# Layer 0's strips regrouped by head, and one ring of eight wide buffers, in a two-layer graph-attention kernel

## The chip, the cores and the metric

The kernel runs on one core of a Trainium2 chip. The metric is the device time in microseconds (us) from the first to the last instruction of one execution. The kernel before took 4317.61 us, the median of three runs (4312.24 to 4321.88). The execution that was recorded with a profile took 4314.55 us, and its span in the trace is 4312.8 us; all times of instructions below are from that execution.

## The reference

Eight graphs of 2048 nodes with 256 features go through two attention layers, each with a residual and a layer norm. All graphs share one adjacency matrix.

```python
def layer0(x, adj, prior, W, a_src, a_dst, beta_tilde, W_out):      # prior = adj here
    x_proj = jnp.einsum('bnd,hdf->bhnf', x, W)                      # 8 heads of 32
    e_src = jnp.einsum('bhnf,hf->bhn', x_proj, a_src)
    e_dst = jnp.einsum('bhnf,hf->bhn', x_proj, a_dst)
    e = leaky_relu(e_src[..., :, None] + e_dst[..., None, :], 0.2)
    e = e + (softplus(beta_tilde) * jnp.log(prior + 1e-6))[:, None, :, :]
    attn = softmax(where(adj > 0, e, finfo.min))
    h = jnp.einsum('bhij,bhjf->bhif', attn, x_proj)
    return h.transpose(0, 2, 1, 3).reshape(B, N, D) @ W_out.T
def layer1(x, adj, W1, W2, W3):
    e = leaky_relu((x @ W1) @ (x @ W2).T, 0.2)
    attention = softmax(where(adj > 0, e, -1e12))
    return relu(attention @ (x @ W3))
x = layernorm(x + layer0(x, ...)); x = layernorm(x + layer1(x, ...))
```

## The kernel before

Layer 0 is done with the scores transposed: the neighbours j lie on the partitions, the queries i along the free axis. The heads are taken in pairs (`hp`, four per graph), and the neighbours in 16 tiles of 128 (`jt`). One pair with one tile is a strip (`step`, from L343), and there are 64 strips per graph, 512 in all. For each of its two heads, called a and b below, a strip makes a weight tile `s` of 128 x 2048 on VectorE (L378): the larger of a query row `c` and a neighbour factor `re`, times the masked prior `mt`. Then TensorE multiplies with it: `products` (L407) adds into the accumulator `val` (128 x 1024, two PSUM banks) with the projected features `v` as weights 32 columns wide, and into `den` with the neighbour factors alone, for the softmax's divisor. The four column groups of the array work side by side: group q has head q % 2 and half q // 2 of its queries, and each of the two banks holds 512 of those 1024 queries. So every round of four matmuls, one per group, reads the tiles of both heads.

For some strips (the table `SUMMED`, by graph and pair) the divisor isn't summed on TensorE. There, ScalarE starts two tiles `d` with a scaled copy of `s` (L395), VectorE adds the later ones of the chain (L389), and in the pair's last strip TensorE reduces both tiles at once with weights of ones. The `d` tiles have two buffers.

After a pair's last strip, `finish` (L414) empties the accumulators with ScalarE: two copies of 64 x 1024 take `val` into `ht` (L423), which holds all heads' rows of a graph as node tile by feature, and one copy of 128 x 1024 takes `den` (L426). The rest of `finish` goes on in later strips: reciprocals by way of HBM (`rec_d`), their rows broadcast back (`rb`, 128 x 1024), and every second pair a multiplication of `ht` by them (L452). `val` and `den` have one buffer each, so the next pair's first matmuls wait for these copies.

When the four pairs of a graph are done, `output` (L455) takes groups of four node tiles through the output projection (`y`, L480), adds the input rows into the same columns of `ht` (L482), and normalizes them there (L483 to L489). A group has two `y` tiles. `turn` (L494) transposes the result into `x1t` and makes layer 1's values `h3`. Layer 1 (`Dot`) then takes 16 rows of 128 queries. A row's scores `e` go through ScalarE into `p` (L545), VectorE adds the mask and takes the row's extreme (L548), ScalarE applies exp in place (L551), and in the next row's turn TensorE transposes `p` (`pt`, L569), with ScalarE copying each transpose out (L571), and multiplies by `h3` into `acc` (L585). The tile `p` is one buffer of 128 x 2048 for the whole kernel.

The tiles `s` rotate through six buffers of 128 x 2048. At the start the same buffers hold the input rows and the tiles `m` from which `mt` is made. Tiles named "mm" (`y`, `e`, `pt`, `tr` and the like) rotate through three PSUM banks.

The first graph's layer 0 runs alone (0 to about 480 us), with the other graphs' projections in between. From then on layer 1 of one graph is interleaved with layer 0 of the next. The order on TensorE is the program's own, and that on the SyncE queue from the second part on; on VectorE and ScalarE a scheduler fixes the order when the program is built. The interleaving puts 4 + 2 strips of the next graph ahead of the output stage, 2 after each of its first groups, then 2 + 2, and the other 44 over 13 rows of layer 1, three or four after each row's `acc`. A graph's strips 16, 32, 48 and 64 end a pair. Strip 16 is followed by transposes and by the start of layer 1; strips 32 and 48 are followed at once by strips of the next pair; strip 64 is followed by a row of layer 1. The last graph's layer 1 runs alone from about 4000 us.

Of the kernel before, what the change touches and what calls it, by code (L numbers as in the profile page):

```python
# [27 lines left out]
def kernel(  # L28
# [40 lines left out]
    SUMMED += [[(2, 4, 10, 13)] + [tuple(range(0, NT, 2))] * (NP - 1)] * (B - 2)  # L69
# [10 lines left out]
    p_all = whole.tile([P, N], F32, tag="p", name="p")  # L80

    def mm_tile(name):
        return ps.tile([P, BK], F32, tag="mm", name=name)

# [42 lines left out]
    first_x = [wide.tile([P, NT // 2, D], F32, tag="s", name="xr", bufs=6) for _ in range(2)]  # L127
# [36 lines left out]
    rec_d = dram.tile([B, NP // 2, 2, 2, 2, HALF], F32, name="rec_d")  # L164
# [8 lines left out]
    def transpose_x(xg, dst):  # L173
        for kc in range(KC):
            t = mm_tile("tr")
            for k in range(IG):
                nc.tensor.transpose(t[:, ts(k, P)], xg[:, k, ts(kc, P)], ident)
            nc.scalar.copy(dst[:, kc, :], t)  # L178

    def make_m(jt):  # L180
# [3 lines left out]
        m = wide.tile([P, NT, P], F32, tag="s", name="m", bufs=6)  # L184
# [51 lines left out]
    class Gat:  # L236
# [12 lines left out]
        def scores_first(self, xt):  # L249
# [3 lines left out]
            for kc in range(KC):  # L253
                for q in range(NB):
                    nc.tensor.matmul(t[ts(q, DH), :], wp[:, kc, D:], xt[:, kc, ts(q, BK)],
                                     start=(kc == 0), stop=(kc == KC - 1))
# [8 lines left out]
        def row(self, it, xt, v, scores=True):  # L265
# [3 lines left out]
            for kc in range(KC):  # L269
                nc.tensor.matmul(t[:, 0:cols], xt[:, kc, ts(it % IG, P)], wp[:, kc, 0:cols],  # L270
# [72 lines left out]
        def step(self, count=1):  # L343

            for _ in range(count):
# [29 lines left out]
                for a in range(HP):  # L375
                    h = hp * HP + a
                    sa = wide_tile("s", "s", 6)
# [13 lines left out]
                self.products(self.val, [v[:, jt, ts(a, DH)] for a in range(HP)], s, jt == 0, jt == NT - 1)  # L391
# [4 lines left out]
                if jt not in chain:  # L396
                    self.products(self.den, [e[:, jt, h:h + 1].to_broadcast([P, DH]) for h in heads], s,
                                  jt == min(set(range(NT)) - set(chain)),
                                  not chain and jt == NT - 1)
                if chain and jt == NT - 1:  # L400
                    self.products(self.den, [ones] * HP, self.sums, False, True)
# [5 lines left out]
        def products(self, dst, weights, s, start, stop):  # L407
            for c in range(HALF // BK):
                for q in range(4):
                    nc.tensor.matmul(dst[ts(q, DH), ts(c, BK)], weights[q % 2],  # L410
                                     s[q % 2][:, ds(q // 2 * HALF + c * BK, BK)],
                                     start=start, stop=stop)

        def finish(self, hp):  # L414
# [4 lines left out]
            if hp == 0:  # L419
                self.ht = whole.tile([P, NT, KC, P], F32, tag="heads", name="ht")  # L420
            ht = self.ht[:, :, hp // 2, :]
            for s in range(2):
                nc.scalar.copy(ht[lo:lo + HP * DH, ts(s, NT // 2), :],  # L423
                               self.val[ts(s, HP * DH), :].rearrange("p (t i) -> p t i", i=P))
# [8 lines left out]
            for s in range(2):  # L433
                nc.sync.dma_start(rec_d[b, hp // 2, s, hp % 2].rearrange("a (p c) -> (a p) c", c=HALF // DH),
# [5 lines left out]
            for s in range(2):  # L440
# [4 lines left out]
                for a in range(2 * HP):  # L445
                    nc.sync.dma_start(rb[ts(a, DH), :],
                                      rec_d[b, hp // 2, s, a // HP, a % HP:a % HP + 1, :].to_broadcast([DH, HALF]))
                rbs.append(rb)
                yield
            for s, rb in enumerate(rbs):  # L450
                half = ht[:, ts(s, NT // 2), :]
                nc.vector.tensor_mul(half, half, rb.rearrange("p (t i) -> p t i", i=P))  # L452
                yield

        def output(self):  # L455
# [13 lines left out]
            for g in range(NB):  # L469
# [5 lines left out]
                z = self.ht[:, ts(g, IG)].rearrange("p t k i -> p t (k i)")  # L475
                for k in range(0, IG, 2):
# [269 lines left out]
```

## Time and profile before

| what | us |
|---|---|
| median of three runs | 4317.61 |
| the profiled execution | 4314.55 |
| its span in the trace | 4312.8 |
| first graph's layer 0 alone | 0 to about 480 |
| each of seven stages with `y`, `turn` and strips | about 100 |
| last graph's layer 1 alone | about 4000 to the end |
| one `s` on VectorE (L378), 1024 of them | 2.342 |
| one copy 64 x 1024 out of `val` (L423), 64 of them | 1.007 |
| one copy 128 x 1024 out of `den` (L426), 32 of them | 1.012 |
| one copy 128 x 512 out of PSUM (L571), 512 of them | 0.583 |

How to read it: a matmul of the program stands as two records in the trace, so that a strip's eight `val` matmuls are sixteen records. Four records, one for each column group, start within 0.03 us of each other, and the next four 0.43 us later. Sixteen therefore take 4 x 0.43 = 1.72 us, though the mean of one record is printed as about 0.6 us. The busy share of TensorE counts such overlapping records once. A wait is put down to the engine whose signal came last.

### The profile page before, as it was taken

What the parts mean: (1) busy time and instruction counts of PE and PEld (TensorE: products, weight loads), DVE (VectorE), ACT (ScalarE), POOL (GpSimd) and SP (SyncE); (2) the same over time, 40 slices, a digit from 0 to 9 for tenths busy, and PEclk for the clock granted to TensorE, in tenths of its full rate; (3) what the DMA queues carried; (4) which work ended last, traced back from release to release, by engine and by line L of the source; (5) the groups of instructions that cost most, each with busy time, mean ns of one, the idle gap of its engine ahead of it and who ended that gap; (6) DMA issues with size and microseconds to landing.
All of it is one profiled execution on the core that took longest, in us unless ns stands there. A gap on an engine that the chain in (4) does not pass through costs nothing.

```text
span 4312.8 us, 58556 instructions
## 1 busy us (share of the span) xinstructions
PE 4174.6 (97%) x24640; PEld 2225.8 (52%) x24640; DVE 3712.1 (86%) x2468; ACT 1634.4 (38%) x3019; POOL 9.5 (0%) x14
## 2 busy tenths in 40 slices
PE   7899999999999999999999999999999999999999
PEld 4444455454555545554555554555455545554766
DVE  6878878998899999999999998999899999998222
ACT  6522143333334333332433333343333334433554
POOL 0000000000000000000000000000000000000000
PEclk9999999999999999999999999999999999999999
DMA  7988856656555564556554565555645565554211
GB/s 238 306 279 301 281 194 220 217 217 219 195 192 193 188 216 179 181 192 214 201 192 172 184 221 185 194 192 197 216 172 181 191 215 197 197 180 141 80 50 41
DMA packets 267943, 843.47 MB, mean 196 GB/s; under 512 B 32672, under 2 KB 165792, under 8 KB 193952
## 3 DMA queue, kind: packets, MB, share of 16 engines
q1 hardware_dynamic: 232352, 806.17, 53.3%
q10 hardware_dynamic: 35328, 33.56, 2.3%
q8 instruction: 193, 3.16, 0.3%
q14 instruction: 70, 0.57, 0.0%
HBM read 763.76 MB, written 75.37 MB: 195 GB/s over the span
## 4 chain that ended last, share of the span: by engine, by line
PE 62%; DVE 20%; issue 8%; DMA 6%; ACT 3%; SPq 0%; ACTq 0%; DVEq 0%; POOLq 0%; POOL 0%
PE acc L585 15%; PE e L543 14%; PE val L410 13%; DVE s L378 13%; PE den L410 9%; PE pt L569 4%; DVE d L389 3%; DMA mt<-mt_d 3%; PE proj L270 2%; DMA c<-c_d 2%; PE h1p L532 2%; PE y L480 2%; DVE p L548 1%; PE h3p L511 1%; DVE ht L482 1%
## 5 line engine op out<-in xcount | busy, mean ns | idle before, releaser
L378 DVE SCALAR_TENSOR_TENSOR s<-c,re,mt 128x2048 f32<-128x2048 f32 x1024 | 2361.2, 2342 | 193.8 <-PE den L410 68.6
L410 PE MATMUL val<-s,v 128*32 128x512 f32 x8192 | 1030.7, 604 | 78.9 <-DVE s L378 77.7
L543 PE MATMUL e<-x1t,h 128*128 128x512 f32 x2048 | 963.6, 594 | 15.2 <-ACT h L534 7.7
L585 PE MATMUL acc<-h,pts 128*128 128x256 f32 x4096 | 905.0, 379 | 0.0
L585 PEld LDWEIGHTS acc<-h,pts 128*128 128x128 f32 x4096 | 777.6, 190 | 156.6 <-issue 57.4
L389 DVE SCALAR_TENSOR_TENSOR d<-s,re,d 128x2048 f32<-128x2048 f32 x318 | 738.1, 2339 | 2.7 <-ACT d L395 2.7
L410 PE MATMUL den<-s,re 128*32 128x512 f32 x5216 | 675.0, 598 | 0.0
L410 PEld LDWEIGHTS val<-s,v 128*32 128x32 f32 x8192 | 257.0, 110 | 695.2 <-issue 515.6
L543 PEld LDWEIGHTS e<-x1t,h 128*128 128x128 f32 x2048 | 350.8, 190 | 278.6 <-issue 248.4
L545 ACT ACTIVATE p<-e 128x512 f32<-128x512 f32 x512 | 305.6, 597 | 463.2 <-PE e L543 452.7
L548 DVE CUSTOM_DVE_ANT_0 p<-p,pen 128x2048 f32<-128x2048 f32 x128 | 292.4, 2284 | 173.1 <-ACT p L545 173.0
L551 ACT ACTIVATE p<-p,neg 128x2048 f32<-128x2048 f32 x128 | 256.5, 2004 | 454.5 <-DVE neg L548 454.5
L571 ACT COPY pts<-pt 128x512 f32<-128x512 f32 x512 | 296.1, 583 | 290.5 <-PE pt L569 285.0
L569 PEld LDWEIGHTS pt<-ident,p 128*128 128x128 f32 x2048 | 245.7, 140 | 286.3 <-issue 250.5
L410 PEld LDWEIGHTS den<-s,re 128*32 128x32 f32 x5216 | 184.6, 112 | 401.0 <-issue 398.1
L569 PE MATMUL pt<-ident,p 128*128 128x128 f32 x2048 | 309.4, 275 | 2.9 <-ACT p L551 2.2
L226 ACT ACTIVATE f<-mv,eps_ln 128x1 f32<-128x1 f32 x128 | 37.8, 295 | 336.8 <-DVE mv L224 336.8
L270 PE MATMUL proj<-wp,xt 128*128 128x272 f32 (+1 forms) x512 | 130.8, 400 | 3.8 <-ACT xt L178 2.3
L591 DVE TENSOR_TENSOR z<-z,x1r 128x256 f32<-128x256 f32 x128 | 53.9, 421 | 82.3 <-ACT z L590 82.2
L272 ACT COPY v<-proj 128x256 f32<-128x256 f32 x128 | 47.2, 374 | 204.0 <-PE proj L270 163.0
L511 PE MATMUL h3p<-w3s,x1t 128*128 128x256 f32 x512 | 122.4, 382 | 1.7 <-ACT x1t L506 1.7
L590 ACT ACTIVATE z<-acc,rec 128x256 f32<-128x256 f32 x128 | 60.2, 471 | 160.5 <-PE acc L585 124.3
(88 smaller groups left out, 1996.9 us busy)
## 6 DMA issues: line engine op xcount, KB each, us to landing
mt<-mt_d SPq DMA_DIRECT2D x496, 1024.0 KB
c<-c_d SPq DMA_DIRECT2D x64, 1024.0 KB
pen<-pen_d SPq DMA_DIRECT2D x112, 512.0 KB
xg<-in_x_dram SPq DMA_DIRECT2D x60, 512.0 KB
adj_t<-in_adj_dram SPq DMA_DIRECT2D x16, 1024.0 KB
mt_d<-mt SPq DMA_DIRECT2D x16, 1024.0 KB
rb<-rec_d SPq DMA_DIRECT2D x128, 128.0 KB
x_d<-ht ACTq DMA_DIRECT2D x32, 512.0 KB
```

The source lines that it names most:

```text
L270: nc.tensor.matmul(t[:, 0:cols], xt[:, kc, ts(it % IG, P)], wp[:, kc, 0:cols], start=(kc == 0), stop=(kc == KC - 1))
L378: nc.vector.scalar_tensor_tensor(sa, self.cs[a], self.re[:, 0, jt, h:h + 1], mt, ALU.max, ALU.mult)
L389: nc.vector.scalar_tensor_tensor(d, sa, e[:, jt - 1, h:h + 1], d, ALU.mult, ALU.add)
L410: nc.tensor.matmul(dst[ts(q, DH), ts(c, BK)], weights[q % 2], s[q % 2][:, ds(q // 2 * HALF + c * BK, BK)], start=start, stop=stop)
L511: nc.tensor.matmul(t[:, ts(i, D)], x1t[:, kc, ts(2 * (j - lag) + i, P)], w3s[:, kc, :], start=(kc == 0), stop=(kc == KC - 1))
L543: nc.tensor.matmul(t, self.h1[:, kc, ts(it % IG, P)], self.x1t[:, kc, ts(c, BK)], start=(kc == 0), stop=(kc == KC - 1))
L545: nc.scalar.activation(p[:, ts(c, BK)], t, AF.Prelu, alpha=ALPHA)
L548: nc.vector.tensor_tensor_reduce(p, p, pen, -1.0, FMAX, ALU.add, ALU.min, neg)
L551: nc.scalar.activation(p, p, AF.Exp, bias=neg, scale=-1.0, accum_out=den)
L569: nc.tensor.transpose(t[:, ts(k, P)], p[:, ts(g * IG + k, P)], ident)
L571: nc.scalar.copy(pt, t)
L585: nc.tensor.matmul(acc, pts[g][:, ts(k, P)], self.h3[:, j, :], start=(j == 0), stop=(j == NT - 1))
```

## The change

A strip's products are regrouped. `products` now takes one head: its four column groups hold the four quarters (512 queries) of that head's rows, all with the same weights, and the head's sums lie in one of the two banks of `val` and `den`. A strip does head a's `val` and `den` products, then head b's.

`ht` becomes two tiles of 128 x 2048, features by nodes, one for each two pairs. The first keeps a place of its own. The second is taken from the wide ring. `finish` takes each of the eight pieces of `val` (32 x 512) to its place with a copy of its own. The layout of `rec_d` and the broadcast of `rb` follow.

In `output`, a group's normalized rows overwrite the 512 columns of its nodes in both tiles of `ht`. All eight matmuls of a group's two `y` tiles now come first, then both additions; and the rows are written to HBM in two DMAs of 256 KB for each group in place of one of 512 KB. `x1(j)` names the place of two node tiles.

The tag of the wide buffers gets eight places (`ring_tile`) where `s` had six, with the tile `p` that was separate now taken from it for each graph's layer 1. The bytes are the same: 6 + 1 + 2 tiles of 8 KB before, 8 + 1 after.

`SUMMED` for the first pair of the graphs from the third on is (0, 4, 10, 13) where it was (2, 4, 10, 13).

```diff
-    SUMMED += [[(2, 4, 10, 13)] + [tuple(range(0, NT, 2))] * (NP - 1)] * (B - 2)
+    SUMMED += [[(0, 4, 10, 13)] + [tuple(range(0, NT, 2))] * (NP - 1)] * (B - 2)
-    p_all = whole.tile([P, N], F32, tag="p", name="p")
+    def ring_tile(name, shape=(P, N)):
+        return wide.tile(list(shape), F32, tag="s", name=name, bufs=8)
...
-                    sa = wide_tile("s", "s", 6)
+                    sa = ring_tile("s")
...
-                self.products(self.val, [v[:, jt, ts(a, DH)] for a in range(HP)], s, jt == 0, jt == NT - 1)
                 if jt in chain[:1]:
                     self.sums = [wide_tile("d", "d", 2) for _ in heads]
                     for d, sa, h in zip(self.sums, s, heads):
                         nc.scalar.activation(d, sa, AF.Copy, scale=e[:, jt, h:h + 1])
-                if jt not in chain:
-                    self.products(self.den, [e[:, jt, h:h + 1].to_broadcast([P, DH]) for h in heads], s,
-                                  jt == min(set(range(NT)) - set(chain)),
-                                  not chain and jt == NT - 1)
-                if chain and jt == NT - 1:
-                    self.products(self.den, [ones] * HP, self.sums, False, True)
+                for a, h in enumerate(heads):
+                    self.products(self.val, a, v[:, jt, ts(a, DH)], s[a], jt == 0, jt == NT - 1)
+                    if jt not in chain:
+                        self.products(self.den, a, e[:, jt, h:h + 1].to_broadcast([P, DH]), s[a],
+                                      jt == min(set(range(NT)) - set(chain)), not chain and jt == NT - 1)
+                    if chain and jt == NT - 1:
+                        self.products(self.den, a, ones, self.sums[a], False, True)
...
-        def products(self, dst, weights, s, start, stop):
-            for c in range(HALF // BK):
-                for q in range(4):
-                    nc.tensor.matmul(dst[ts(q, DH), ts(c, BK)], weights[q % 2],
-                                     s[q % 2][:, ds(q // 2 * HALF + c * BK, BK)],
-                                     start=start, stop=stop)
+        def products(self, dst, a, weights, s, start, stop):
+            for q in range(NB):
+                nc.tensor.matmul(dst[ts(q, DH), ts(a, BK)], weights, s[:, ts(q, BK)], start=start, stop=stop)
...
-                self.ht = whole.tile([P, NT, KC, P], F32, tag="heads", name="ht")
-            ht = self.ht[:, :, hp // 2, :]
-            for s in range(2):
-                nc.scalar.copy(ht[lo:lo + HP * DH, ts(s, NT // 2), :],
-                               self.val[ts(s, HP * DH), :].rearrange("p (t i) -> p t i", i=P))
+                self.ht = [whole.tile([P, N], F32, tag="heads", name="ht")]
+            elif hp == HP:
+                self.ht.append(ring_tile("ht"))
+            ht = self.ht[hp // HP]
+            for a in range(HP):
+                for q in range(NB):
+                    nc.scalar.copy(ht[ds(lo + a * DH, DH), ts(q, BK)], self.val[ts(q, DH), ts(a, BK)])
...
-                z = self.ht[:, ts(g, IG)].rearrange("p t k i -> p t (k i)")
-                for k in range(0, IG, 2):
-                    y = mm_tile("y").rearrange("p (t c) -> p t c", t=2)
-                    for i in range(2):
-                        for kc in range(KC):
-                            nc.tensor.matmul(y[:, i, :], self.ht[:, g * IG + k + i, kc, :], wot[:, kc, :],
-                                             start=(kc == 0), stop=(kc == KC - 1))
-                    nc.vector.tensor_add(z[:, k:k + 2, :], y, xs[g][:, k:k + 2, :])
-                    nc.vector.bn_stats(st[:, k // 2, :], z[:, k:k + 2, :].rearrange("p t c -> p c t"))
+                ys = [mm_tile("y").rearrange("p (t c) -> p t c", t=2) for _ in range(2)]
+                for k in range(IG):
+                    for kc in range(KC):
+                        nc.tensor.matmul(ys[k // 2][:, k % 2, :], self.ht[kc][:, ts(g * IG + k, P)], wot[:, kc, :],
+                                         start=(kc == 0), stop=(kc == KC - 1))
+                z = [self.x1(2 * g + k) for k in range(2)]
+                for k in range(2):
+                    nc.vector.tensor_add(z[k], ys[k], xs[g][:, ts(k, 2), :])
+                    nc.vector.bn_stats(st[:, k, :], z[k].rearrange("p t c -> p c t"))
...
-                nc.scalar.dma_start(x1_d[b].rearrange("(t p) d -> p t d", p=P)[:, ts(g, IG), :], z)
+                    if k % 2:
+                        nc.scalar.dma_start(x1_d[b].rearrange("(t p) d -> p t d", p=P)[:, ts(2 * g + k // 2, 2), :],
+                                            z[k // 2])
+        def x1(self, j):
+            return self.ht[j % 2][:, ts(j // 2, BK)].rearrange("p (t c) -> p t c", t=2)
...
-            self.p = p_all
+            self.p = ring_tile("p")
```

## The prediction

> **What bounds the kernel now.** I read the page's busy shares first, then the chain that ended last, then the waits of the two busiest engines, and then the same things by stage.
>
> ```profile
> PE 4174.6 (97%) x24640; PEld 2225.8 (52%) x24640; DVE 3712.1 (86%) x2468; ACT 1634.4 (38%) x3019; POOL 9.5 (0%) x14
> PE 62%; DVE 20%; issue 8%; DMA 6%; ACT 3%; SPq 0%; ACTq 0%; DVEq 0%; POOLq 0%; POOL 0%
> PE val L410 <- DVE s L378: 77.7, 64, 5.5
> PE e L543 <- ACT h L534: 7.7, 6, 2.2
> PE val L410 <- ACT ht L423: 1.0, 2, 0.7
> DVE s L378 <- PE den L410: 68.6, 38, 3.7
> ```
>
> TensorE is the bound, but its one large wait, 77.7 us in 64 pieces, is for VectorE's `s`; and VectorE waits 68.6 us for a free `s` buffer. The two engines hold each other up by turns. The wait for the copies out of `val` is 1.0 us in all. By stage, with one output stage (2510 to 2610 us) and one stretch of layer 1's rows (2620 to 2980 us), where the columns are length, then PE, PEld, DVE, ACT and POOL busy, clock and DMA:
>
> ```profile
> 2510.00:2610.00 100.00, 93.26 (x581) 49.70 (x578) 89.61 (x60) 31.35 (x59) 0.00 (x0) 0.97 0.64 223
> 2620.00:2980.00 360.00, 356.25 (x2043) 188.50 (x2046) 344.34 (x218) 130.77 (x235) 0.00 (x0) 1.00 0.52 184
> ```
>
> In the rows both engines are over 95% busy. In the output stage neither is full and the clock drops. From 2500 to 2616 us TensorE waits 6.5 us for `s`, from 2616 to 3000 us 2.3 us. So what can be had on TensorE is about 9 us a graph over seven graphs, plus 14.3 us in the first graph's layer 0 (3.5 + 4.9 + 5.9 in its three windows). The last thing I read is the end of a pair, in the timeline:
>
> ```profile
> 1359.11 1.93 PE L410 MATMUL val<-s,v 128*32 128x512 f32 x16
> 1360.85 1.90 PE L410 MATMUL den<-s,re 128*32 128x512 f32 x16
> 1361.10 2.03 ACT L423 COPY ht<-val 64x1024 f32<-64x1024 f32 x2 [1.41 <-PE val L410]
> 1362.57 1.90 PE L410 MATMUL den<-d,ones 128*32 128x512 f32 x16
> 1364.29 3.62 PE L410 MATMUL val<-s,v 128*32 128x512 f32 x32
> 1366.02 1.01 ACT L426 COPY dn<-den 128x1024 f32<-128x1024 f32 x1 [0.49 <-ACT z L230]
> ```
>
> `val` is complete at T + 1.72 (T = 1359.11), its copies end at T + 4.0, and TensorE, busy with `den` until T + 5.18, starts the next pair without a pause. The margin is 1.2 us.
>
> **What the Trainium skill says.** "Perfetto Trace Analysis", Identifying Performance Opportunities: the same gap repeating on the engine that should be full can mean too few buffers. The 64 and 38 waits above agree. "TensorEngine Tiling (Array Packing)", PSUM Bottleneck: tiling speeds up the array but not the emptying of PSUM, and PSUM reads are to be widened over tiles of one bank; the change goes the other way. "ScalarE: Activation LUTs", What ACT_TABLE_LOAD costs: an instruction without pointer operands costs 186 ns plus 0.833 ns an element, and back to back they overlap by about 93 ns. That gives 613 ns for 512 elements; the trace has 583, and 2.05 us for four in a row, so I use the trace. "TensorE: Matmul & The Clock Gate", What's Actually Happening: after an idle window of about 3.4 us the clock is halved. The trace agrees in kind: 0.97 in the output stage, 1.00 in the rows.
>
> **The change, part by part.**
>
> Products by head. Counts and round times stay: 16 + 16 records a strip, 0.43 us for four. What moves is the start. Before, the first round needs both heads' `s`, and VectorE makes them 2.34 us apart. Now a's half runs in that time, and only b's half comes after the later `s`. It pays where TensorE waits for VectorE. In the output stage VectorE sets the end: its last `s` there ends at 2593.5 and TensorE still has `val`, `den` and the reduction to do, 3 x 1.72 = 5.16 us. Half of that, 2.58, goes: 7 x 2.58 = 18 us. Of the 2.3 us of waits in the rows I take half: 7 x 1.2 = 8 us. In the first graph the waits are up to 5.5 us and a den strip can save at most 1.72 of each; I take 6 of 14.3 us.
>
> Ring of eight. `p` holds one place during layer 1, and the second half of `ht` one from the end of the third pair to the end of `turn`, so `s` gets seven, then six; eight only in the first graph. Before it was six. VectorE's 5.1 us of buffer waits in the rows (2616 to 3000) can't reach the end whole, because TensorE is as full; below I price this at nothing beyond the 8 us just counted. The built order of VectorE does change: the first masked row (L548) of each layer 1 now stands before two strips that preceded it. That makes exp earlier where TensorE waited for it (1.6 us once in 2616 to 3000, less in the other graphs): I take 1 us, 7 in all. VectorE then idles until that row's scores are out; it is made up only if its lead lasts, and this is in the range.
>
> Output stage. Each first addition now waits for 16 records of `y` instead of 8 (1.8 us later), since it overwrites rows that the second tile reads. VectorE waits 3.5 us for `y` a stage today. In the built order an `s` stands ahead of both additions where the first addition stood, which covers it. I take a gain of 1 us a stage, 7. If that cover fails, the loss is up to 4 x 1.8 us a stage, 50 us. The second DMA of each group is 0.37 us of issuing on ScalarE (the median of its 32 issues), 32 times, behind the normalization, on no path.
>
> End of a pair. Eight copies of 32 x 512 cost as much as any 512-element copy: four take 2.05 us, eight 7 x 0.515 + 0.58 = 4.2 us, for 2.03 before; 32 x 2.2 = 69 us more on ScalarE, which is 38% busy. In the built program the first copy waits for the last `val` matmul of both heads, and the next pair's first matmul waits for the eighth copy: the banks aren't released one by one. Head b's `val` now ends later, at T + 3.44, as a's `den` and reduction (0.86 each) come before it. So the copies run from T + 3.7 to T + 7.9, and TensorE, done at T + 5.16, waits 2.8 us where it had a margin. At strip 32 a `d` copy (2.0 us, can't start before a's reduction at T + 2.58) stands ahead of them on ScalarE: T + 9.1, a stall of 3.9 us, of which about 1.1 is a wait for the transposes' copy that the old order had a little later; 2.8 net. Strips 32 and 48 have this, 5.6 us a graph. VectorE isn't held up by it unless it runs out of places, and it is at 95%: what it gets ahead in the stall shortens the next waits for `s`. I let half through: 7 x 2.8 = 20 us. At strip 16 transposes follow, and their copies come out of the queue some 0.6 us too late: 4 us. At strip 64 the copies end 1.1 us later counted from the last `s`, but TensorE's own work after it is 2.58 shorter: nothing. First graph, three pair ends, with projections between that need ScalarE: 1 us each, 3 us. Last output stage, with no strips to cover the later addition: 2 us.
>
> `SUMMED`. The chain of the first pair starts at strip 0 instead of 2: as many products and additions; `den` of the new pair starts one strip later, which keeps its copy (now last behind eight) off the path. Nothing.
>
> DMA: `rb` in runs of 2 KB instead of 4 KB, 128 transfers of 128 KB each. DMA is at 0.52 to 0.64 and these land strips ahead. Nothing.
>
> Sum: gains 18 + 8 + 6 + 7 + 7 = 46; losses 20 + 4 + 3 + 2 = 29; net -17. From the profiled 4314.55 that is 4297.5. The median of the runs is 3 us above it, so I forecast 4300 us.
>
> **Rivals.**
>
> Slower: the whole-tile release at a pair's end. If VectorE, nearly full itself, can't turn the stall into a lead, TensorE pays 2.8 + 2.8 at strips 32 and 48, 0.6 at 16, and 2.2 at strip 64 (where the last `s` isn't late, the transposes' copies queue behind T + 7.9 and `den`'s): 8.4 x 7 = 59 us. With 5 for first graph and tail, against gains of 40: +24, about 4341 us. It decides from 6.6 us a graph, where the gains of 46 are used up. For it: the next pair's strips follow at once. Against: TensorE's and VectorE's waits show that neither is ever far ahead.
>
> Even: the two engines at 95% bound each other, each gain on one is a wait on the other: 4312 to 4326 us.
>
> Much faster: waits of both kinds shrink by more, with the half-clock stretches of the output stage. All of the 77.7 less the pair ends' 20: about 4250 us. Against: in that stage VectorE's work is the bound, and no part of it gets less.
>
> **How the numbers follow.** Forecast 0.42, much faster 0.08, even 0.16, slower 0.34. About 0.2% (8.6 us) is what a measurement of this kernel tells from no change. Faster 0.50, same 0.16, slower 0.34. The range reaches from the much faster case to just over the slower one: 4256 to 4348. The forecast's own range is 4275 to 4309.
>
> **What would show it.** Right: TensorE's wait for `s` falls from 77.7 to about 40; one 4.2 us block of copies a pair; waits of `val` for the copies of `ht` of 40 to 80 us, new; output stages about 3 us shorter. The slower case: that wait at 40 or more, with VectorE's waits for buffers or scores grown as well. Wrong altogether: additions waiting for `y` (31.3 us today) at 80, or rounds of products longer than 0.43 us.

## The result, and the profile after

The changed kernel took 4391.65 us (median of four runs, 4390.38 to 4400.31) against 4319.1 for the kernel before on the same chip: ratio 1.0175, interval 1.0157 to 1.0193. It is slower by some 73 us, and the forecast of 4300 has the wrong sign. The profiled execution has a span of 4390.9 us, 78 more than before.

The page after, the busy shares and the chain that ended last:

```profile
PE 4163.8 (95%) x24640; PEld 2221.5 (51%) x24640; DVE 3697.2 (84%) x2468; ACT 1714.5 (39%) x3211; POOL 7.5 (0%) x14
PE 62%; DVE 19%; issue 6%; ACT 6%; DMA 3%; SPq 0%; ACTq 0%; DVEq 0%
```

TensorE and VectorE both lose two points of their share. In the chain ScalarE has doubled, from 3 to 6%. That engine is busy for 39% of the span only; what it does matters where others wait for it. The waits of TensorE and VectorE say where (who waits, for what; us in total, times, longest):

```profile
PE val L414 <- ACT ht L428: 74.1, 14, 9.6
PE val L414 <- DVE s L382: 48.2, 40, 2.7
PE e L554 <- ACT pts L582: 21.6, 8, 6.5
DVE s L382 <- PE den L414: 19.7, 13, 4.5
```

Two of the waits that the change could shorten did shorten: TensorE's for `s` from 77.7 to 48.2 us, VectorE's for a free buffer from 68.6 to 19.7. But the first products of a new pair now wait 74.1 us for the copies that empty `val`, in 14 pieces (strips 32 and 48 of seven graphs), where that wait was 1.0. And the scores wait longer for the transposes' copies, 21.6 us (7.5 before).

Parts of the timeline at strip 32 of the fifth graph, then at strip 48 (start, length, engine, line, operation, and in brackets the idle time before it with what ended it):

```profile
2774.36 2.33 DVE L382 SCALAR_TENSOR_TENSOR s<-c,re,mt 128x2048 f32<-128x2048 f32 x1
2774.80 1.04 PE L414 MATMUL val<-s,v 128*32 128x512 f32 x8
2776.52 1.04 PE L414 MATMUL den<-d,ones 128*32 128x512 f32 x8
2776.62 0.17 DVE L228 BATCH_NORM_AGGREGATE mv<-st 128x2 f32<-128x6 f32 x1
2777.72 0.60 ACT L234 ACTIVATE z<-z,f 128x256 f32<-128x256 f32 x1
2778.22 1.99 ACT L398 ACTIVATE d<-s,re 128x2048 f32<-128x2048 f32 x1
2780.23 3.51 ACT L428 COPY ht<-val 32x512 f32<-32x512 f32 x6
2783.76 1.17 ACT L428 COPY ht<-val 32x512 f32<-32x512 f32 x2
2784.98 3.64 PE L414 MATMUL val<-s,v 128*32 128x512 f32 x16 [7.42 <-ACT ht L428]
...
2909.82 1.04 PE L414 MATMUL val<-s,v 128*32 128x512 f32 x8
2910.92 4.71 ACT L428 COPY ht<-val 32x512 f32<-32x512 f32 x8 [0.47 <-PE val L414]
2915.68 4.24 PE L414 MATMUL val<-s,v 128*32 128x512 f32 x24 [3.11 <-ACT ht L428]
```

At strip 48 nothing stands ahead of the copies: they start as soon as `val` is complete, take 4.71 us, and the next product begins 0.05 us after the last. TensorE is idle for 3.11 us. At strip 32 `val` is complete at 2775.84 but ScalarE is not free for it until 2780.23: a layer normalization, which itself waited for VectorE's `mv` (queued behind an `s` of 2.33 us), and then a `d` copy of 1.99 us come first. TensorE is idle for 7.42 us. In the other six graphs the stall at strip 32 is 6.8 to 9.6 us, and at strip 48 it is 3.11 in all seven.

Look at the length of the products after the stall: 16 records take 3.64 us, where the same took 1.93 at the pair's end shown of before. The clock has halved. A table by window shows it for the 7 us after the stall (the columns are those of the table by stage in the prediction; the clock is third from the end):

```profile
2770.00:2785.00 15.00, 7.58 (x71) 2.16 (x69) 13.63 (x10) 9.53 (x18) 0.00 (x0) 0.90 0.34 123
2785.00:2792.00 7.00, 7.00 (x30) 2.78 (x31) 3.04 (x3) 4.30 (x5) 0.00 (x0) 0.72 0.43 153
2792.00:2915.00 123.00, 120.57 (x699) 64.46 (x698) 111.06 (x74) 45.35 (x87) 0.00 (x0) 1.00 0.51 179
```

The trace's record of the clock holds 73.6 us at half clock before and 153.3 after (mean clock 0.992 and 0.983), with new stretches behind the pairs' ends of every graph. Of these 80 us more, 62 fall where TensorE is busy (58 before, 120 after). At half speed it gets half as much done, so up to 62 / 2 = 31 us are lost that no wait shows. This is what "TensorE: Matmul & The Clock Gate" of the Trainium skill, section What's actually happening, describes (idle for about one window of 3.4 us, then half clock); here even the stall of 3.11 us was followed by it.

An account: copies' wait +73.1, scores' wait +14.1, half clock up to +31, wait for `s` -29.5: +89 at most, where the span grew by 78. Smaller waits are left out, and TensorE's busy time moved for another reason too (see the part on the products by head below), so this is right in its order and no closer. By place it is clear. Call an output stage the time from its first `y` product to the first masked row of layer 1, and the rows the time from there to the next `y`. The seven output stages together went from 630 to 619 us, the seven stretches of rows from 2876 to 2961. Strips 32 and 48 lie in the rows, so the loss is where the stalls are.

### The profile page after: what moved, and what is told of

Same layout as the page of the kernel before. It is cut to its first block, busy times and chain, and to the rows that moved or that the text cites. A ratio compares the mean times of both kernels' runs of the same rounds, so it can differ in the third digit from the quotient of the medians.

```text
span 4390.9 us, 58737 instructions
## 1 busy us (share of the span) xinstructions
PE 4163.8 (95%) x24640; PEld 2221.5 (51%) x24640; DVE 3697.2 (84%) x2468; ACT 1714.5 (39%) x3211; POOL 7.5 (0%) x14
## 4 chain that ended last, share of the span: by engine, by line
PE 62%; DVE 19%; issue 6%; ACT 6%; DMA 3%; SPq 0%; ACTq 0%; DVEq 0%
PE e L554 15%; PE acc L596 15%; PE val L414 13%; DVE s L382 11%; PE den L414 8%; DVE d L393 4%; PE pt L580 4%; ACT ht L428 3%; PE h1p L543 2%; PE y L483 2%; DMA mt<-mt_d 2%; PE proj L274 2%; DVE p L559 1%; PE h3p L522 1%; ACT d L398 1%
## 5 line engine op out<-in xcount | busy, mean ns | idle before, releaser
L414 PE MATMUL val<-s,v 128*32 128x512 f32 x8192 | 1039.4, 609 | 122.7 <-ACT ht L428 74.1
L554 PE MATMUL e<-x1t,h 128*128 128x512 f32 x2048 | 974.1, 600 | 22.7 <-ACT pts L582 21.6
L414 PE MATMUL den<-s,re 128*32 128x512 f32 x5216 | 684.5, 597 | 0.0
L414 PEld LDWEIGHTS val<-s,v 128*32 128x32 f32 x8192 | 243.6, 111 | 716.5 <-issue 480.4
L414 PEld LDWEIGHTS den<-s,re 128*32 128x32 f32 x5216 | 169.9, 111 | 393.6 <-issue 393.6
L428 ACT COPY ht<-val 32x512 f32<-32x512 f32 x256 | 147.8, 577 | 129.8 <-PE val L414 127.0
L602 DVE TENSOR_TENSOR z<-z,x1r 128x256 f32<-128x256 f32 x128 | 53.9, 421 | 89.1 <-ACT z L601 89.1
L483 PE MATMUL y<-wot,ht 128*128 128x256 f32 x512 | 123.4, 396 | 1.9 <-ACT x1t L517 1.9
```

The costliest lines, as they stand in the source:

```text
L414: nc.tensor.matmul(dst[ts(q, DH), ts(a, BK)], weights, s[:, ts(q, BK)], start=start, stop=stop)
L428: nc.scalar.copy(ht[ds(lo + a * DH, DH), ts(q, BK)], self.val[ts(q, DH), ts(a, BK)])
L554: nc.tensor.matmul(t, self.h1[:, kc, ts(it % IG, P)], self.x1t[:, kc, ts(c, BK)], start=(kc == 0), stop=(kc == KC - 1))
```

## The experiments

Theory R: `val` is one tile of two banks, so the next pair's first product waits for all eight copies; what counts is how long the copies, and what stands ahead of them on ScalarE, hold the tile past the time for which TensorE has other work. Rival N: eight copies are too much for ScalarE however the tile is freed. Rival G: the moved order of VectorE, the ring or the output stage is the cause. Rival C came later: not the copies but the cover lost through the by-head order (cover is the work that TensorE still has between `val`'s last product and the next pair's first).

All results first. Ratios are to the kernel before on the same chip; the three columns after them are from the profiled run: TensorE's wait of `val` for the copies, its wait for `s`, and the mean clock. The order on VectorE and ScalarE is fixed anew for each build, so an edit can move other instructions as well.

| kernel | median us | ratio, interval | for copies | for `s` | clock |
|---|---|---|---|---|---|
| changed kernel | 4391.65 | 1.0175, 1.0157 to 1.0193 | 74.1 | 48.2 | 0.983 |
| split_val | 4306.95 | 0.9966, 0.9954 to 0.9979 | 13.0 | 69.3 | 0.991 |
| ring_only | 4325.62 | 1.0015, 1.0009 to 1.0022 | 20.0 | 66.9 | 0.992 |
| regroup_only | 4379.19 | 1.0133, 1.0115 to 1.0151 | 66.8 | 40.2 | 0.986 |
| before_eight | 4358.61 | 1.0081, 1.0058 to 1.0104 | 22.9 | 75.0 | 0.990 |
| regroup_split | 4307.38 | 0.9971, 0.9961 to 0.9980 | 29.4 | 47.9 | 0.992 |
| two_copies | 4319.06 | 1.0000, 0.9992 to 1.0009 | 35.5 | 57.3 | 0.990 |
| vals_first | 4330.87 | 1.0025, 1.0016 to 1.0035 | 40.0 | 53.1 | 0.990 |
| split_both | 4311.43 | 0.9984, 0.9976 to 0.9992 | 30.8 | 51.7 | 0.990 |
| chain_late | 4374.25 | 1.0130, 1.0114 to 1.0145 | 46.5 | 57.8 | 0.986 |
| split_vals_first | 4299.64 | 0.9953, 0.9940 to 0.9965 | none | 57.2 | 0.993 |
| svf_chain_late | 4357.36 | 1.0088, 1.0073 to 1.0104 | none | 90.4 | 0.990 |
| sums_from_2 | 4400.66 | 1.0188, 1.0172 to 1.0203 | 71.7 | 45.2 | 0.980 |

**split_val**: the changed kernel, with `val` as two tiles of one bank, one for each head. Each head's bank is free after its own four copies.

```diff
-                    self.val = pacc.tile([P, HALF], F32, tag="val", name="val")
+                    self.val = [pacc.tile([P, BK], F32, tag=f"val{a}", name=f"val{a}") for a in range(HP)]
-                    self.products(self.val, a, v[:, jt, ts(a, DH)], s[a], jt == 0, jt == NT - 1)
+                    self.products(self.val[a], 0, v[:, jt, ts(a, DH)], s[a], jt == 0, jt == NT - 1)
-                    nc.scalar.copy(ht[ds(lo + a * DH, DH), ts(q, BK)], self.val[ts(q, DH), ts(a, BK)])
+                    nc.scalar.copy(ht[ds(lo + a * DH, DH), ts(q, BK)], self.val[a][ts(q, DH), :])
```

> The changed kernel, but val is two tiles of one bank each, one per head, instead of one tile of two banks; nothing else. Theory R (the one tile is freed only after all eight copies): the waits of val for the copies of ht fall from 74.1 us to under 15 and most of the time comes back, 4310 to 4345 us. Theory N (eight copies are too much for ScalarE however val is freed): the waits move to the transposes' copies and it stays above 4370. Theory G (the regrouped order on VectorE, with more waits for layer 1's scores, sets the time): 4380 to 4392.

The same eight copies, the same matmuls, and 85 us less, a little more than was expected. The rows take 74 us less together than with the change (2887), the output stages 8. Parts of the timeline of its strip 32:

```profile
2727.91 2.35 ACT L428 COPY ht<-val 32x512 f32<-32x512 f32 x4 [1.99 <-PE val L414]
2729.38 1.04 PE L414 MATMUL val<-s,v 128*32 128x512 f32 x8
2730.28 2.00 ACT L398 ACTIVATE d<-s,re 128x2048 f32<-128x2048 f32 x1
2731.95 1.04 PE L414 MATMUL val<-s,v 128*32 128x512 f32 x8
2732.31 2.34 ACT L428 COPY ht<-val 32x512 f32<-32x512 f32 x4
2734.70 1.06 PE L414 MATMUL val<-s,v 128*32 128x512 f32 x8 [1.71 <-ACT ht L428]
```

Head a's four copies end at 2730.26, before head b's last products of `val`, which start at 2729.38, are done. The next pair's first product (2731.95) writes a's bank although b's copies begin only at 2732.31. The stall is 1.71 us, and the eight records after it take 1.06 us: full clock. "PSUM — Partial Sum Buffer" of the Trainium skill, section The four PSUM rules, has each bank as a memory of its own. The trace agrees: b's bank is being emptied from 2732.31 on while a's is written until 2732.99. The tile, not the bank, was what tied them together. Rival N falls: ScalarE does no less work here.

**ring_only** and **regroup_only** take the change apart. ring_only has the ring of eight, the shared weight buffers, the new `ht` and the new output stage, with the old strips and two copies. regroup_only is the kernel before with strips by head and eight copies into the old `ht`. In short:

```diff
 ring_only, from the changed kernel: products, rec_d, rb and SUMMED as before;
-            for a in range(HP):
-                for q in range(NB):
-                    nc.scalar.copy(ht[ds(lo + a * DH, DH), ts(q, BK)], self.val[ts(q, DH), ts(a, BK)])
+            for s in range(2):
+                nc.scalar.copy(ht[lo:lo + HP * DH, ts(s, HALF)], self.val[ts(s, HP * DH), :])
 regroup_only, from the kernel before: products, rec_d and rb as in the change;
-            for s in range(2):
-                nc.scalar.copy(ht[lo:lo + HP * DH, ts(s, NT // 2), :],
-                               self.val[ts(s, HP * DH), :].rearrange("p (t i) -> p t i", i=P))
+            for a in range(HP):
+                for q in range(NB):
+                    nc.scalar.copy(ht[ds(lo + a * DH, DH), ts(q, IG), :],
+                                   self.val[ts(q, DH), ts(a, BK)].rearrange("p (t i) -> p t i", i=P))
```

> The ring of eight, the two ht tiles, p in the ring and the output stage of the change, with the old strips (two heads in each round, two copies of 64 x 1024, the old chain). R and N: no stall at the ends of pairs, 4295 to 4325 us, at or a little under the kernel before. G, if the ring's order or the later additions are the cause: over 4350.

> The kernel before with the strips regrouped by head and eight copies into the old ht; six s buffers, p apart, the old output stage and chain. R and N: 4375 to 4420 us, the stalls at the ends of pairs are all there. G (ring or output stage as cause): 4310 to 4335.

The ring and the output stage alone cost 6 us, the regrouping alone 59 of the change's 73. Rival G falls as the main cause. But ring_only was expected to have no stall at the ends of pairs, and it has seven, all at strip 32, of 1.2 to 5.3 us (20.0 in all) for its two copies. In its fifth graph `val` is complete at 2740.65 and the copies start at 2746.35, behind a normalization whose inputs stood behind two `s` on VectorE. So the new order on VectorE stalls strip 32 even without the products by head. In regroup_only the wait for the copies is there in the same 14 pieces.

**before_eight**: the kernel before, old order, with eight copies in place of two.

```diff
-            for s in range(2):
-                nc.scalar.copy(ht[lo:lo + HP * DH, ts(s, NT // 2), :],
-                               self.val[ts(s, HP * DH), :].rearrange("p (t i) -> p t i", i=P))
+            for q in range(4):
+                for c in range(2):
+                    nc.scalar.copy(ht[ds(lo + q % 2 * DH, DH), ds(q // 2 * (NT // 2) + c * IG, IG), :],
+                                   self.val[ts(q, DH), ts(c, BK)].rearrange("p (t i) -> p t i", i=P))
```

> The kernel before, with val emptied by eight copies of 32 x 512 instead of two of 64 x 1024; the products stay as they were. N: 4370 us or more. R: val is complete 1.7 us earlier than by head, so the copies end at about T + 6.6 against T + 5.2 where TensorE is done: stalls of 1.5 to 3 us at strips 32 and 48, 4335 to 4365.

Copies alone, with the old cover of 3.44 us of `den` products: 39 us, about half of the change's loss. The wait for the copies is 22.9 us, 0.95 at each strip 48 and 1.7 to 3.7 at strip 32 (1.5 to 3 expected at both). The rows are 22 us longer together than before, which fits it; the output stages are 16 us longer, and why is not known.

The copies themselves are faster here than in the change, 4.26 us for eight:

```profile
2767.77 4.26 ACT L424 COPY ht<-val 32x512 f32<-32x512 f32 x8 [0.41 <-ACT z L230]
```

The last section comes back to this.

**two_copies** and **vals_first** ask which of the two ends of the stall matters, the copies' length or the cover. two_copies is the changed kernel with two copies. It leaves out that each head's rows get to their own place in `ht`: they land elsewhere, so its output is not the layer's, but the work is otherwise the same. vals_first is the changed kernel with eight, but both heads' `val` products first.

```diff
 two_copies
-            for a in range(HP):
-                for q in range(NB):
-                    nc.scalar.copy(ht[ds(lo + a * DH, DH), ts(q, BK)], self.val[ts(q, DH), ts(a, BK)])
+            for s in range(2):
+                nc.scalar.copy(ht[lo:lo + HP * DH, ts(s, HALF)], self.val[ts(s, HP * DH), :])
 vals_first
-                for a, h in enumerate(heads):
+                for a in range(HP):
                     self.products(self.val, a, v[:, jt, ts(a, DH)], s[a], jt == 0, jt == NT - 1)
+                for a, h in enumerate(heads):
                     if jt not in chain:
```

> The changed kernel with two copies of 64x1024 in place of eight of 32x512, val still one tile of two banks. The heads' rows land in other places of the heads' tile, so the output differs from the reference; the work is the same otherwise. Theory R: what counts is how long the copies hold the tile. Two take 2.0 us, eight 4.7, so each of the stalls at strips 32 and 48 shrinks by 2.7 us (7.4 to 4.7 and 3.1 to 0.4): the waits of val for the copies fall from 74 to about 37 us, half clock from 153 to about 110, the time to 4325 to 4355 us. Rival C (the number of copies is a side matter; what counts is that the by-head order left nothing between the last product of val and the next pair's first): the waits stay over 60 us and the time over 4370.

> The changed kernel with one order changed: within a strip both heads' products of val come first, then both heads' of den, as in the kernel before. val is one tile, with eight copies. At a pair's end some 2.1 us more of den's products stand between the last product of val and the first of the next pair. Theory R with cover: each stall shrinks by that 2.1 us (7.4 to 5.3, 3.1 to 1.0): waits of val for the copies 45 us, time 4345 to 4370. Rival C (the lost cover is the whole cause): waits under 15 us and 4310 to 4325. If the stalls come from what ScalarE does ahead of the copies and not from when val is done: no change, 4385 to 4395.

Both are faster than expected. Strip 48 is the clean place, since nothing stands ahead of the copies there. In two_copies:

```profile
2867.40 2.03 ACT L427 COPY ht<-val 64x1024 f32<-64x1024 f32 x2 [0.46 <-PE val L414]
2869.48 1.92 PE L414 MATMUL val<-s,v 128*32 128x512 f32 x16 [0.43 <-ACT ht L427]
```

In vals_first, strip 32 and then strip 48:

```profile
2749.36 3.35 PE L415 MATMUL val<-s,v 128*32 128x512 f32 x16 [4.12 <-ACT ht L429]
...
2878.80 2.78 PE L415 MATMUL val<-s,v 128*32 128x512 f32 x24 [1.57 <-ACT ht L429]
```

The stall at strip 48 is 3.11 with the change, 0.43 with 2.7 us less of copies (0.4 was expected), 1.57 with 1.7 us more of cover (1.0 was expected). It is the copies' length less the cover, as R has it, and neither part alone is the cause: rival C expected waits of over 60 us in two_copies and under 15 in vals_first. At strip 32 of two_copies 6.09 us remain in this graph and 3.3 to 4.8 in the six others (4.7 expected), from what stands ahead on ScalarE. Against the change the rows are 54 us shorter in two_copies and 44 in vals_first; another 7 and 20 us are gained in the output stages, where these stalls are not, and vals_first's 20 stay open. After the stall of 0.43 us 16 records take 1.92 us: no halved clock.

**chain_late**: the changed kernel, with no `d` copy at the first strip of the second to fourth pairs.

```diff
-    SUMMED += [[(0, 4, 10, 13)] + [tuple(range(0, NT, 2))] * (NP - 1)] * (B - 2)
+    SUMMED += [[(0, 4, 10, 13)] + [(2, 4, 6, 8, 9, 10, 12, 14)] * (NP - 1)] * (B - 2)
```

> The changed kernel with val still one tile, but the second to fourth pairs' summed strips (2, 4, 6, 8, 9, 10, 12, 14) in place of (0, 2, ... 14): as many products and additions, but no d copy at a pair's first strip. At strip 32 of the changed kernel a d copy of 2.0 us stood on ScalarE ahead of the eight copies (2778.22 to 2780.21, then 2780.23 to 2784.92). If ScalarE's queue ahead of the copies is part of the stall, strip 32's wait falls from 7.4 to about 5.4, strip 48's (where the d copies stand after) stays: waits of val for the copies 74 to about 60 us, half clock 153 to about 130, the time 4365 to 4380 us. If the layer normalization ahead of the d copy alone holds the copies, or the d copies then delay something else: 4387 to 4396.

The timeline at strips 32 and 48:

```profile
2770.59 1.94 PE L414 MATMUL val<-s,v 128*32 128x512 f32 x8 [3.09 <-ACT ht L428]
...
2902.44 1.06 PE L414 MATMUL val<-s,v 128*32 128x512 f32 x8 [3.11 <-ACT ht L428]
```

Both stalls are now the copies alone. So 4.3 of strip 32's 7.42 us was ScalarE's queue, more than the 2.0 us of the `d` copy itself: the order as built anew has the normalization behind the copies as well (it starts at 2771.48). The time is in the expected range, but not for the expected reason. The wait for the copies fell by 27.6 us, and yet the rows, where it lies, are 10 us longer together; the output stages are 27 us shorter. So the wait at strip 32 shows what ScalarE's queue held up, and the time of this run does not show what that was worth. Neither shift was traced.

**regroup_split** is regroup_only with `val` in two tiles as in split_val; **split_both** is split_val with `den` in two tiles too.

```diff
 split_both
-                    self.den = pacc.tile([P, HALF], F32, tag="den", name="den")
+                    self.den = [pacc.tile([P, BK], F32, tag=f"den{a}", name=f"den{a}") for a in range(HP)]
-            nc.scalar.copy(dn, self.den)
+            for a in range(HP):
+                nc.scalar.copy(dn[:, ts(a, BK)], self.den[a])
```

> The kernel before with strips by head and eight copies into the old ht tiles (the regrouping alone, 4379 us), and with val as two tiles of one bank. There is no ring of eight, no shared weight buffers and the old choice of summed strips. Theory R (the loss is that val comes free as a whole): the 66.8 us that products of val waited for the copies fall under 20 us, the stretches at half clock from 122 us to about 80, and the time falls by 60 to 85 us, to 4295 to 4320 us. If the ring and the output stage's tiles are worth nothing with this order too (they were worth nothing with the old strips: 4325.6 against 4319.9), it stands within 8 us of the 4307 us that the changed kernel took with val split. If they are worth what the prediction gave them (some 20 us of row and factor waits), it stands at 4320 us or more.

> The changed kernel with val and den both as two tiles of one bank, and den emptied by two copies of 128x512 in place of one of 128x1024. val split alone took 4307 us. Theory R for den too: den's tile is held only until its own half is copied; but no wait of den's products for its copy shows in any trace so far, and two copies cost ScalarE about 0.1 us more at each of 32 pair ends, so no more than 3 us either way: 4304 to 4310. If den's release still held the first product of den in the next pair behind the waits for val (hidden by them in the trace), the gain is 5 to 10 us: 4297 to 4302.

regroup_split and split_val stand at the same ratio, 0.9971 and 0.9966. With `val` split, the ring of eight, the shared buffers, the new output stage and `SUMMED` are together worth nothing that can be told. The wait for the copies didn't fall under 20 us as expected (29.4), and the time was met all the same. Splitting `den` too gains nothing: split_both is just over its range, and it waits longer for the copies (30.8 us, against 13.0 in split_val), which was not traced.

**split_vals_first** and **svf_chain_late** add vals_first's order, and then chain_late's sums, to split_val. **sums_from_2** is the changed kernel with `SUMMED` as it was.

```diff
 sums_from_2
-    SUMMED += [[(0, 4, 10, 13)] + [tuple(range(0, NT, 2))] * (NP - 1)] * (B - 2)
+    SUMMED += [[(2, 4, 10, 13)] + [tuple(range(0, NT, 2))] * (NP - 1)] * (B - 2)
```

> The changed kernel with val as two tiles and both heads' val products first within a strip. vals_first alone (4331 us) had output stages of 84 us from the third graph on, where the others with val split have 86 to 89, but rows of 416; val split alone (4307 us) has rows of 412. If both gains add: 7 x 3 = some 20 us below val split alone, 4282 to 4292. If the short output stage only gave back what the stalls before it had taken (VectorE ahead after them): 4302 to 4311.

> As split_vals_first, with the summed strips (2, 4, 6, 8, 9, 10, 12, 14) for the second to fourth pairs. If the d copy is the last thing that still holds the copies at strip 32, the remaining waits of val for the copies (13 us in all with val split) go, and the time is 3 to 15 us below split_vals_first. If two additions in a row on VectorE (after strips 8 and 9) cost more waits for s than that: 0 to 15 us above it.

> The changed kernel with the first pair's summed strips of the third graph on back at (2, 4, 10, 13). The prediction priced this edit at nothing. If so: within 8 us of the changed kernel, 4384 to 4399. If the d copies at strip 0, after the output stage, are on the path: 4 us and more a graph less, under 4370. If starting at strip 2 puts d copies or den's products in the way: above 4400.

split_vals_first is the fastest median of all and beats both kernels; its interval overlaps that of split_val, so which of these two is faster is not settled. It lies between its two expected ranges. No wait of `val` for the copies is left in its trace:

```profile
PE val L415 <- DVE s L382: 57.2, 43, 4.4
PE e L555 <- ACT pts L583: 28.7, 19, 2.0
```

svf_chain_late missed its expectation by far, and on the instructive side. Without a sum at a pair's first strip, `den` of the new pair is needed in that strip, and `den` is still one tile whose copy stands last behind the eight. Strip 32 in its timeline:

```profile
2759.70 3.64 PE L415 MATMUL den<-s,re 128*32 128x512 f32 x16 [3.60 <-ACT dn L431]
```

The stall and the halved clock (3.64 us for 16 records) are back, one tile further on: 18.6 us in six pieces. The wait for `s` rose by 33 us too, as the two additions in a row might explain; that was not separated. sums_from_2 can't be told from the changed kernel: the intervals overlap, though its median is 9 us higher and just over the 4400 from which harm was expected.

## Why the prediction was wrong

The mechanism was in it, on both sides of the balance; its price was wrong in three terms, and all three went one way. Of its signs, the wait for the copies of 40 to 80 us came true (74.1), but it stood for the forecast and for the slower case alike. The slower case asked besides for longer waits of VectorE. Those for the scores of a masked row did grow, from 173 to 287 us, but they are 255 in split_val too, which lost nothing. So neither sign measures the loss.

**The step that failed is "End of a pair", "I let half through: 7 x 2.8 = 20 us".** First, the stall's size: priced at 2.8 + 2.8 = 5.6 us a graph, measured at 7.42 + 3.11 = 10.5. Strip 48 was near. Its copies took 4.7 us and not the 4.2 of the sum. The sum's pitch of 0.515 us is about 2.05 us divided by four copies; from one to the next, those 128-partition copies are 0.49 us apart. The copies of 32 partitions follow each other at 0.585 in the order of the change, and only in another order (before_eight) do eight take 4.26. Strip 32 was not near. I put the `d` copy at the earliest moment at which its operands are ready and took ScalarE as free by then; but the normalization ahead of it in ScalarE's order waits for VectorE's `mv`, and that now stands behind one more `s`. chain_late's stall puts ScalarE's queue there at 4.3 us.

Second, "half". The reason given, that what VectorE gets ahead shortens the next waits for `s`, is real but smaller. From the changed kernel to split_val the stall falls by 61 us and the wait for `s` rises by 21: a third was given back. From regroup_only to regroup_split it is 37 and 8, a fifth.

Third, the clock. The prediction has halving only in the output stage. A stall on an engine that is otherwise full costs its own length and then up to half of each 3.4 us stretch behind it: up to 31 us here, two thirds of all the gains. The rival on the slower side had the same mechanism and "decides from 6.6 us a graph", which was right, but at 8.4 us a graph with no clock it gave 4341.

**Strip 64, "nothing".** Wrong too. The scores there wait for the transposes' copies behind the eight copies and `den`'s, as the rival had it with 2.2 us. Parts of the timeline of the changed kernel:

```profile
3027.81 4.69 ACT L428 COPY ht<-val 32x512 f32<-32x512 f32 x8 [11.23 <-PE val L414]
3032.53 1.01 ACT L430 COPY dn<-den 128x1024 f32<-128x1024 f32 x1
3033.81 0.59 ACT L582 COPY pts<-pt 128x512 f32<-128x512 f32 x1
3034.45 3.54 PE L554 MATMUL e<-x1t,h 128*128 128x512 f32 x4 [2.24 <-ACT pts L582]
```

2.24 us of wait, and the four matmuls behind it take 3.54 us where the same took 1.88 a few microseconds before: again the clock.

**Products by head and output stage, a gain of 18 + 8 + 6 + 7.** The sign holds once the stall is out of the way, the size doesn't. An output stage, measured from its first `y` product to the first masked row, has a median of 89.5 us before, 89.1 with the change and 87.0 in split_val: 2.5 x 7 = 17.5 us instead of 25. A graph's rows in split_val take 412.8 us against 411.2 (medians), so nothing of the 8 us is seen there. On TensorE itself more was gained: from before to split_val, which have the same time at half clock where it is busy (58 and 59 us), its busy time falls by 35 us (4174.6 to 4139.2). regroup_split has 4140.6, and ring_only, with the old strips, 4173.8, so it goes with the order by head. But its idle time rises by 32 us, much as the even rival had it: what one engine gains, it waits for on the other. Part of the 35 us may be waits themselves, since a wait inside a round of the old order is in part drawn as work (at 2591.27 of before, two records are drawn as 1.04 us of work ahead of 1.18 us of waiting for `s`). The additions did not wait longer for `y` (28.3 us against 31.3), as forecast, and the wait for `s` fell in the direction that was named, to 48.2 instead of about 40.

**Ring of eight, "nothing beyond the 8 us".** Right to within what ring_only shows (+6 us with the old strips, interval 1.0009 to 1.0022) and regroup_split against split_val (no difference). VectorE's buffer waits did fall, from 68.6 to 30.2 us in ring_only, and its waits for the scores of a masked row rose from 173 to 261: idle time that moved from one cause to another. **`SUMMED`, "nothing"**: nothing that sums_from_2 can tell, and no product of `den` waits for the copy in its trace. The reason given, keeping `den`'s copy off the path, is worth having in the other pairs, as svf_chain_late shows. **Last output stage, a loss of 2.** It went from 40.4 to 43.0 us, as forecast.

What stays open: why output stages take 84 us in vals_first and split_vals_first from the third graph on and 83 to 85 in chain_late, but 86 to 94 elsewhere, with the longest in before_eight; and what made chain_late's rows longer.

## What to carry to other kernels

A stall at the end of a tile's life is the time from its last write to the end of everything that reads it, less the other work that the writer has in the meantime; before it is multiplied by the number of ends, walk the reader engine's queue as it is built, with what that queue itself waits for. If a tile of two banks is emptied in pieces, make it two tiles: here that turned 1.75% of loss into 0.34% of gain with the same copies. And on a TensorE that is full otherwise, count a stall of 3 us as some 5 (3.11 and half of a 3.41 us stretch, here), because the clock may halve behind it; of the stalls here, a fifth to a third came back.

## What the runs showed of the hardware

Copies out of `val` of 32 partitions don't get cheaper with fewer partitions, and in the order of the change they didn't overlap. By shape, in the changed kernel:

```profile
L428 ACT COPY ht<-val 32x512 f32<-32x512 f32 x256 | 147.8, 577 | 129.8 <-PE val L414 127.0
```

And in the kernel before:

```profile
L423 ACT COPY ht<-val 64x1024 f32<-64x1024 f32 x64 | 64.5, 1008 | 99.1 <-PE val L410 96.2 <-ACT z L230 2.5
```

The mean is 577 ns for 512 columns of 32 partitions and 1008 for 1024 columns of 64: a quarter of the elements for 57% of the time. "ScalarE: Activation LUTs" of the Trainium skill, What ACT_TABLE_LOAD costs, gives 186 + 0.833 x 512 = 613 ns for one and some 93 ns of overlap from one to the next. The trace has 577 for one, and eight of the change take 4.71 us, 0.585 apart: no overlap. In before_eight one takes 575 ns, and the overlap is there for some. Its order empties both banks of one group of 32 partitions before it goes on to the next group. Where a copy reads the same partitions as the one before it, the two start 0.48 us apart, which is 93 ns of overlap; where it reads others, they start 0.58 apart, though the bank changes there too. In the change every copy reads other partitions than the one before it. Four copies of 128 partitions, 0.49 apart, fit this. What the engine does in between is not shown, and copies of the same partitions in the same bank did not occur here.

The clock's record shows when a stall is paid for twice. In the traces of all fourteen kernels nearly every stretch at half clock lasts 3.41 us or two, three or four times that. A product of `val` or `den` waited for one of ScalarE's copies 149 times at a pair's end. None of the 48 such stalls under 2 us had a stretch at half clock between its start and 2 us after its end; 8 of the 20 between 2 and 3 us had one, 24 of the 27 from 3.0 to 3.2, and 53 of the 54 longer ones.
